# Four-layer network on one core: the expert layer's gathers ordered behind norms, its rows fetched one turn earlier, its one-hots in buffers of their own

## The chip, the core and the metric

The kernel runs on one core of a Trainium2 chip. It is one program of four layers. The metric is the device time of an execution in microseconds; below, "us" counts from the start of the span of the profiled execution. The engines are TensorE (PE, with its weight loads PEld), VectorE (DVE), ScalarE (ACT), GpSimd (POOL) and SyncE (SP, which issues most of the plain DMAs). Each engine executes its own instructions in order, and waits on semaphores for the others.

## The reference

The input x has 4 sequences of 512 tokens of 256 features (`[4, 512, 256]`, here called sequences 0 to 3). Each layer normalises x and adds a mixer and a feed-forward part, both of the same normalised x:

```python
xn = _layernorm(x, axis=-1)
x = x + _L1_attn_ref(xn) + _L1_ffn_ref(xn, ...)
xn = _layernorm(x, axis=-1)
x = x + _L2_attn_ref(xn, ...) + _L2_ffn_ref(xn, ...)
```

The change touches layer 1's end and layer 2's start. Layer 1 has dilated attention (segments of 64 tokens, every second token, 16 heads of 16 features) and a mixture of 32 experts, of which each token takes its best 4:

```python
logits = x @ gate_w.T + gate_b
topk_logits, topk_idx = jax.lax.top_k(logits, K)          # K = 4 of E = 32
topk_weight = jax.nn.softmax(topk_logits, axis=-1)
...                                                        # tokens sorted by expert
gate = jnp.minimum(ragged_dot(xt, w_gate) + b_gate, 7.0)
up = jnp.clip(ragged_dot(xt, w_up) + b_up, -7.0, 7.0)
activated = (up + 1.0) * (gate * sigmoid(1.702 * gate))
outs = ragged_dot(activated, w_down) + b_down
y = sum over the token's 4 experts of outs * topk_weight
```

Layer 2 has a gated linear attention with 16 heads (`_chunk_abc`, weights Wq, Wk, Wv, Wg, Ws, Wo) and a latent attention with 8 experts. Layer 3 is causal attention and another mixture of experts.

## The kernel before

x stays in SBUF as 16 tiles of 128 tokens by 256 features, four to a sequence. `xn` has the same shape and holds the normalised tokens; `xnT` holds them with features on the partitions. The program's order on each engine's queue is fixed when it is built: a scheduler takes the instructions in the order the program emits them, by priorities and by what is ready, so the emitted order of neighbouring pieces shapes each queue but does not set it alone.

**The experts of layer 1.** Tokens are written to DRAM (`l_rows`), each expert's tokens are counted and get places in blocks of 128 rows. Work runs in *units* of two blocks. A unit passes five steps: `fetch1` (two indirect gathers, issued by POOL, bring the rows of its two blocks into a tile `r`, line L1313), `features1` (PE transposes them to rt, L1325; ACT copies to rT), `hidden1` (PE gu L1341, DVE and ACT the activation), `product1` (DVE L1355, L1356), `output1` (PE o L1362, ACT y, SP stores to `l_outs`). `Line.turn` issues, for turn n, the features of unit n, the fetch of a unit ahead, the output of unit n−3, the product of n−2 and the hidden part of n−1. The fetch ahead is of unit n+2 (`at(n + 2)`), into one of three tiles `r`. The arm that runs here has 16 turns of blocks that are given to the experts beforehand and 19 of paired blocks, 35 turns between 215 and 361 us; then an arm of single blocks, 7 turns, 366 to 393 us. Beside the turns run pieces of other work: dilated attention chains, and the building of the four weights of each token (`share1`): one-hots `eq` (DVE compares, POOL multiplies at L1238), which use the tag `pvs` of the dilated chains' ACT copies.

**The end of layer 1.** `collect1(b)` adds the expert results to sequence b: 16 indirect gathers (POOL, L1273), each of 128 rows of 256 from `l_outs`, into eight scratch places lying in `xn` and `xnT` of that sequence, each followed by a DVE multiply-add into x (`accumulate`, L532). `collect1(0)` is interleaved with the last two dilated chains: PE sc L1430, ACT e L1433, PE pv L1442, ACT pvs L1447, PE pvt L1451, DVE r L1453, o L1456 and the add to x L1462. Then `layer_norm(0)`: DVE statistics (L438, L439), POOL rs (L427 and L429, a power of −0.5), DVE xn (L457).

**Layer 2.** `normed(b)` runs what is left of `collect1(b)`, then `layer_norm(b)`, then `to_features` (PE tr L472, ACT xnT). The gated attention goes in units u of a pair of heads and a sequence (u mod 4 is the sequence). `run(u)` interleaves the unit's own steps "m", the supply "s" of unit u+1 (its projections PE pj L1664), the drain "d" of unit u−1, and, beside them, a latent chain. While units 0 to 2 run, one or two gathers of `collects[u + 1]` are emitted per step:

```python
for _ in range(2 - (u and n % 2)):
    next(gathered, None)
```

DVE a L1989 is the latent attention's norm (its rms comes from POOL L427 and L429 as well), eF L1674 the first exponent step of a unit, s L1733 a masked product of scores; kT L2034, q L2040 and L2043 (POOL) and junk L2066 belong to the latent attention; POOL L1828, L1832 and L1835 to the gated output's norm. `rsqrt` remembers its last instruction in `self.mark`, which is POOL's L429.

Of the kernel before, what the change touches and what calls it, by code (L numbers as in the profile page):

```python
# [115 lines left out]
class Net:  # L116
# [934 lines left out]
    def layer1(self):  # L1051
        nc, a, moe, r1 = self.nc, self.a, self.moe1, self.r1
        with ExitStack() as ctx:
            tp = lambda n, bufs, **k: ctx.enter_context(self.tc.tile_pool(name=n, bufs=bufs, **k))
            wp = tp("l1w", 1)

            gw, gb, bg, bu1, bd = self.l1w
            more = wp.tile([P, 8, 3, D], F32, tag="more", name="more")
            self.stock += [more[:, :4], more[:, 4:]]
            for g in (2, 3):  # L1060
                self.load_group(g)
            wa, wk = tp("l1a", 2), tp("l1", 3)
            ptr, pg, po, pd = (tp("l1" + n, 2, space=PSUM) for n in ("tr", "g", "o", "d"))
            self.wk1, self.ps1, self.fetched = wk, (ptr, pg, po), {}

            e = wa.tile([P, 16, 4, 32], F32, tag="e", name="e", bufs=1)
            v = wa.tile([P, 2, 8, 32], F32, tag="v", name="v", bufs=1)
            zeros = lambda n: self.hide.unsqueeze(1).to_broadcast([P, n, T])
            nc.scalar.mul(v.rearrange("p c j d -> p (c j d)").unsqueeze(1), zeros(1), 0.0)
            nc.gpsimd.memset(v[:, :, :, 16:17], 1.0)  # L1070
            nc.scalar.mul(e.rearrange("p (i j) s n -> p i (j s n)", j=4), zeros(4), 0.0)

            units = [(b, p) for b in range(NB) for p in range(2)]
            dilated = lambda u: self.dilated(*units[u], e, v, wa, pd, scalar=u < 2 or u > 5)
            early = [dilated(u) for u in range(2)]
            turns = iter([early[0]] * 3 + [early[1]] * 3)
            for _ in self.places1(wk, po):
                chain = next(turns, None)
                if chain:
                    next(chain)  # L1080
            held = [wp.tile([P, 2, D], F32, tag=f"r{i}", name="r") for i in range(2)]
            for i in range(2):
                self.fetch1(2 * i, held[i])
            for chain in early:
                next(chain)
            bias = self.block_bias(wp, wa, ptr, po, (bg, bu1))

            static = lambda t: dict(place=t % 16, bias=(bg[:, t : t + 1], bu1[:, t : t + 1]))
            over = lambda c: tuple(bias[:, m, c : c + 1] for m in range(2))
            pair = lambda j: [dict(place=j if j < 2 else 8 + (j - 2) % 8, bias=over(j))] * 2  # L1090
            single = lambda j: dict(place=(2 + j) % 8, bias=over(32 + j))

            def static_done(n):
                if n % 2 and n < 8:
                    self.load_group(n // 2 + 4)
                if n == 8:
                    for j in range(2):
                        self.load_expert(j, j)
                if n in (10, 11):
                    for j in range(3 * (n - 10), 3 * (n - 10) + 3):  # L1100
                        self.load_expert(2 + j, 32 + j)
                if n >= 12:
                    for j in range(2 * (n - 12), 2 * (n - 12) + 2):
                        self.load_expert(8 + j, 2 + j)

            singles_at = STATIC + 2 * PAIRS
            for pairs in self.arms1(0, [1 + 2 * i for i in range(PAIRS // 2 + 1)]):
                line = Line(self)
                at = lambda n: 2 * n if n < STATIC // 2 + pairs else None
                pieces = self.beside1(bd, wa, ptr, pd, [dilated(u) for u in (2, 3, 4, 5)])  # L1110
                credit, rate = 0.0, 35 / (STATIC // 2 + pairs - 1)
                for n in range(STATIC // 2):
                    line.turn(
                        dict(t=2 * n, n=n, parts=[static(2 * n), static(2 * n + 1)], done=static_done), at(n + 2)
                    )
                    if n in (8, 10):
                        self.fetch1(singles_at + n - 8, held[n // 2 - 4])
                    credit += rate
                    while credit >= 0.999:
                        credit -= 1  # L1120
                        next(pieces, None)

                def pair_done(j):
                    if 2 <= j < pairs - 8:
                        self.load_expert(8 + (j - 2) % 8, j + 8)

                for j in range(pairs):
                    line.turn(dict(t=STATIC + 2 * j, n=j, parts=pair(j), done=pair_done), at(STATIC // 2 + j + 2))
                    credit += rate
                    while credit >= 0.999:  # L1130
                        credit -= 1
                        next(pieces, None)
                line.end(pieces)
            for singles in self.arms1(1, list(range(17))):
                line = Line(self)

                def single_done(k):
                    for j in (2 * k + 8, 2 * k + 9):
                        if j < 2 * singles:
                            self.load_expert((2 + j) % 8, 32 + j)  # L1140

                for j in (6, 7):
                    if j < 2 * singles:
                        self.load_expert((2 + j) % 8, 32 + j)
                for k in range(singles):
                    line.turn(
                        dict(t=singles_at + 2 * k, n=k, parts=[single(2 * k), single(2 * k + 1)], done=single_done),
                        singles_at + 2 * k + 4 if k + 2 < singles else None,
                    )
                line.end(iter(()))  # L1150
            self.latent_loads()
            last = [dilated(u) for u in (6, 7)]
            next(last[0])
            turns = {1: 0, 4: 0, 5: 1, 8: 1, 10: 0, 12: 1}
            for n, _ in enumerate(self.collect1(0)):
                if n in turns:
                    next(last[turns[n]])
            self.layer_norm(0)
            for chain in last:
                for _ in chain:  # L1160
                    pass
        self.routing.close()
        self.stats = self.small
        self.ordered.close()
# [11 lines left out]
    def beside1(self, bd, wa, ptr, pd, chains):  # L1176
# [54 lines left out]
        for m in range(6):  # L1231
            if m > 1:
                nc.vector.tensor_reduce(self.share1[:, :, m - 2], eqs[m - 2], AX.X, ALU.add)
            if m < 4:
                eq = wa.tile([P, 4, P], F32, tag="pvs", name="eq").rearrange("p a b -> p (a b)")
                eqs.append(eq.rearrange("p (i e) -> p i e", e=32))
                nc.vector.tensor_tensor(eqs[m], slot, s8[:, :, m : m + 1].to_broadcast([P, NTILE, 32]), ALU.is_equal)
                nc.gpsimd.tensor_tensor(eqs[m], eqs[m], w, ALU.mult)  # L1238
            yield
# [66 lines left out]
    def fetch1(self, t, r=None):  # L1306

        nc, moe = self.nc, self.moe1
        if r is None:
            r = self.wk1.tile([P, 2, D], F32, tag="r", name="r")  # L1310
        self.fetched[t] = r
        for i in range(2):
            nc.gpsimd.indirect_dma_start(  # L1313
                out=r[:, i, :], out_offset=None, in_=moe["rows"][:, :],
                in_offset=bass.IndirectOffsetOnAxis(ap=moe["in_slot"][:, t + i : t + i + 1], axis=0),
            )
# [164 lines left out]
    def layer2(self):  # L1481
# [8 lines left out]
        with ExitStack() as ctx:  # L1490
# [19 lines left out]

            def normed(b):
                if b:
                    for _ in collects[b]:
                        pass
                    self.layer_norm(b)
                yield
                self.to_features(
                    gp["ps"], self.xn[:, 4 * b : 4 * b + 4, :], self.xnT[:, :, b * T : (b + 1) * T], tag="ps"
# [3 lines left out]
            def run(u, beside, rate):  # L1522
# [7 lines left out]
                order = "mmmmsmsmmdmmsmsdmsd" if u + 1 < UNITS else "mmmmdmmdmmdmmm"  # L1530
                for n, what in enumerate("mmmmmmmdmmmsmsmdssds" if u < NB - 1 else order):
                    next(chains[what], None)
                    for _ in range(2 - (u and n % 2)):
                        next(gathered, None)
                    credit += rate
                    while credit >= 1:
                        credit -= 1
                        next(beside, None)

            collects = {b: self.collect1(b) for b in range(1, NB)}  # L1540
            norms = [normed(b) for b in range(NB)]
            for it in (norms[0], supplied(0)):
# [982 lines left out]
```

## Time and profile before

| | us |
|---|---|
| three timed runs | 2213.72, 2217.41, 2217.51 |
| median | 2217.41 |
| profiled execution, its own time | 2224.51 |
| span of the profiled execution | 2222.8 |
| PE busy in the span | 1959.6 (88%) |
| DVE busy | 1188.3 (53%) |
| ACT busy | 833.8 (38%) |
| POOL busy | 641.3 (29%) |
| gathers of layer 1's results (L1273), 64, first and last start | 397.7, 512.8 |
| one such gather on POOL, median | 0.94 to 0.96 |

The page of a profile gives busy times of the engines, then the span in 40 equal slices with the busy share of each engine in tenths; the chain that ended last; the groups of instructions with the idle time before them and what ended it; and the DMA issues. Beside the page, the trace answers for a window, a line or a tile of the program: what it waited for, and who waited for it. A line such as "POOL rs L429" names engine, tile and line of the kernel.

### The profile page before, as it was taken

Reading aid. Unit: us, or ns where it says so; the run is one execution under the profiler, and the core shown is the slowest. Engines: PE = TensorE matmul, PEld = TensorE weight load, DVE = VectorE, ACT = ScalarE, POOL = GpSimd, SP = SyncE. Lnnn points to the kernel's source line nnn. Section 1 sums busy time; section 2 is a strip of 40 time slices with the busy share of each in tenths; the row PEclk is TensorE's granted clock in tenths of the full one; section 3 lists DMA queues with packets and bytes.
Section 4 is the critical chain, followed back from the end, with each engine's and each line's share of the span. In section 5 each row is a group of like instructions: output and inputs, shape, how many; then the busy total and the mean of one; then the engine's idle time right before and its main releaser. Section 6 shows DMA issues by size and latency. Waiting matters only on the chain.

```text
span 2222.8 us, 35354 instructions
## 1 busy us (share of the span) xinstructions
PE 1959.6 (88%) x13015; PEld 1432.5 (64%) x13015; DVE 1188.3 (53%) x3448; ACT 833.8 (38%) x1681; POOL 641.3 (29%) x748
## 2 busy tenths in 40 slices
PE   5755988158999999999999999999999988899995
PEld 2423877134666676666666676666787866678895
DVE  5747764257465655555555656555655564522223
ACT  1243354221434433434433434334344533334321
POOL 6324573553112112121111121111444352022231
PEclk9955999568999999999999999999899999899998
DMA  8312985430000000000000000001443320167697
GB/s 287 130 38 83 289 257 164 138 90 20 1 18 6 8 11 6 8 10 6 6 13 6 8 11 6 27 11 41 131 125 111 99 81 1 42 229 266 213 329 244
DMA packets 149548, 198.20 MB, mean 89 GB/s; under 512 B 16885, under 2 KB 127576, under 8 KB 149208
## 3 DMA queue, kind: packets, MB, share of 16 engines
q1 hardware_dynamic: 135224, 156.40, 21.8%
q0 software_dynamic: 14112, 39.15, 6.0%
q8 instruction: 111, 1.82, 0.3%
q14 instruction: 101, 0.83, 0.1%
HBM read 154.21 MB, written 41.29 MB: 88 GB/s over the span
## 4 chain that ended last, share of the span: by engine, by line
PE 55%; issue 8%; DVE 8%; POOL 6%; DMA 3%; ACT 2%; another core or an unknown queue 1%; SPq 0%; POOLq 0%; DVEq 0%; ACTq 0%
PE pt L1742 8%; PE pj L1664 6%; PE o L1855 4%; PE kq L2091 3%; PE sc L1727 3%; PE pov L1806 2%; PE g L2276 2%; PE qk L2059 2%; DVE junk L2066 2%; PE pv L2107 2%; DMA r<-l_rows,in_slot 2%; POOL l_outs L383 1%; PE turn L1695 1%; PE st L1715 1%
## 5 line engine op out<-in xcount | busy, mean ns | idle before, releaser
L2066 DVE CUSTOM_DVE_ANT_0 junk<-qk,hide 128x512 f32<-128x512 f32 (+3 forms) x256 | 124.1, 485 | 42.8 <-PE qk L2059 24.5
L2099 POOL TENSOR_SCALAR_AFFINE_SELECT pr<-pr 128x512 f32<-128x512 f32 x64 | 40.3, 642 | 346.6 <-ACT pr L2096 346.6
L2276 PEld LDWEIGHTS g<-rT,we 128*128 128x128 f32 x1120 | 132.2, 194 | 5.3 <-ACT rT L376 3.3
L2276 PE MATMUL g<-rT,we 128*128 128x128 f32 x1120 | 133.0, 278 | 1.7 <-ACT rT L376 1.6
L1742 PE MATMUL pt<-Wg,xnT 128*128 128x256 f32 x512 | 126.9, 401 | 2.6 <-DVE both L361 1.0
L343 POOL DMA_INDIRECT r<-l_rows,in_slot x73 | 71.2, 975 | 191.2 <-PE rt L374 109.0
L383 POOL DMA_INDIRECT l_outs<-y,to x73 | 72.7, 995 | 184.1 <-ACT y L382 152.4
L1855 PE MATMUL o<-Wo,oT 128*128 128x256 f32 x512 | 121.9, 381 | 0.0
L1742 PE MATMUL pt<-Wv,xnT 128*128 128x256 f32 x512 | 120.6, 387 | 0.0
L1733 DVE TENSOR_TENSOR s<-sc,keep 128x512 f32<-128x512 f32 x128 | 82.4, 682 | 66.1 <-PE sc L1727 66.1
L1742 PEld LDWEIGHTS pt<-Wg,xnT 128*128 128x128 f32 x512 | 99.6, 201 | 27.6 <-issue 7.7
L1677 DVE RECIPROCAL rz<-rz 128x128 f32<-128x128 f32 x128 | 116.7, 932 | 0.3
L355 DVE TENSOR_TENSOR mine<-r,number 128x2 f32<-128x2 f32 x73 | 12.8, 175 | 182.0 <-DMA r<-l_rows,in_slot 175.7
L2096 ACT ACTIVATE pr<-kq 128x512 f32<-128x512 f32 (+1 forms) x192 | 86.6, 530 | 53.1 <-PE kq L2091 52.8
L1742 PEld LDWEIGHTS pt<-Wv,xnT 128*128 128x128 f32 x512 | 95.2, 191 | 15.4 <-issue 0.3
L1313 POOL DMA_INDIRECT r<-l_rows,in_slot x84 | 84.5, 1005 | 66.7 <-PE rt L1325 37.3
L1855 PEld LDWEIGHTS o<-Wo,oT 128*128 128x128 f32 x512 | 96.2, 197 | 9.2 <-issue 1.2
L2091 PE MATMUL kq<-q,kT 32*128 32x128 f32 (+3 forms) x512 | 90.3, 485 | 9.7 <-DVE mx L2066 8.1
L1745 ACT COPY v<-pt 128x512 f32<-128x512 f32 x64 | 37.5, 586 | 121.8 <-PE pt L1742 120.7
L2043 POOL TENSOR_TENSOR q<-q 128x512 f32<-128x512 f32 x16 | 20.3, 1267 | 214.4 <-DVE q L2040 214.3
L1823 DVE TENSOR_TENSOR o<-pov,g 128x512 f32<-128x512 f32 x64 | 41.2, 685 | 74.5 <-ACT sq L1822 74.3
L2091 PEld LDWEIGHTS kq<-q,kT 32*128 32x128 f32 x512 | 40.0, 189 | 55.8 <-DVE mx L2066 34.4
(560 smaller groups left out, 4591.9 us busy)
## 6 DMA issues: line engine op xcount, KB each, us to landing
we<-l_w SPq DMA_DIRECT2D x70, 512.0 KB
we<-l_wo SPq DMA_DIRECT2D x35, 512.0 KB
l_outs<-none SPq DMA_DIRECT2D x1, 11776.0 KB
l_outs<-y SPq DMA_DIRECT2D x42, 256.0 KB
we<-l_r_gate SPq DMA_DIRECT2D x38, 128.0 KB
we<-l_r_up SPq DMA_DIRECT2D x38, 128.0 KB
we<-l_r_down SPq DMA_DIRECT2D x38, 128.0 KB
l_rows<-xn SPq DMA_DIRECT2D x8, 544.0 KB
```

The lines of the kernel that those rows point to most:

```text
L343: self.nc.gpsimd.indirect_dma_start(out=r[:, m, :], out_offset=None, in_=moe["rows"][:, :], in_offset=bass.IndirectOffsetOnAxis(ap=moe["in ...
L383: self.no_order(moe["name"] + " back", nc.gpsimd.indirect_dma_start(out=moe["outs"][:, :], out_offset=bass.IndirectOffsetOnAxis(ap=to, axi ...
L1313: nc.gpsimd.indirect_dma_start(out=r[:, i, :], out_offset=None, in_=moe["rows"][:, :], in_offset=bass.IndirectOffsetOnAxis(ap=moe["in_slot ...
L1664: nc.tensor.matmul(ps, w[n][:, k, :], self.xnT[:, k, t["b"] * T : (t["b"] + 1) * T], start=(k == 0), stop=(k == KD - 1))
L1677: inverse = lambda c: nc.vector.reciprocal(rz[:, c * P : (c + 1) * P], rz[:, c * P : (c + 1) * P])
L1733: nc.vector.tensor_tensor(s, ps[hh], keep4, ALU.mult)
L1742: nc.tensor.matmul(ps[:, i, :], self.xnT[:, k, s : s + P], w[n][:, k, :], start=(k == 0), stop=(k == KD - 1))
L1855: nc.tensor.matmul(ps[:, p, :], of_parity(oT[:, h, c * D : (c + 1) * D], p), wo[:, h, :], start=(h == 0), stop=(h == 1),)
L2066: nc.vector.tensor_tensor_reduce(out=junk[:, :m], in0=tiles[j][:, off : off + m], in1=self.hide[:, T - m :], op0=ALU.add, op1=ALU.max, sca ...
L2091: nc.tensor.matmul(tiles[j][:, BLOCK[i] - off : BLOCK[i] - off + T - i * P], kT[r, i * P : (i + 1) * P], qT[r, i * P :], start=True, stop= ...
L2096: nc.scalar.activation(pr[:, j, off : off + m], tiles[j][:, :m], AF.Exp, scale=0.25)
L2276: nc.tensor.matmul(pt[:, m, :], we[:, q, k * T + m * P : k * T + (m + 1) * P], rT[:, k, :], start=(k == 0), stop=(k == KD - 1),)
```

## The change

It has three parts. In the arm of pairs the rows are fetched three turns ahead in place of two, with one more fetch at the start and four tiles `r`. The one-hots `eq` get a tag of their own. And the gathers of sequences 1 to 3 in layer 2 are emitted inside `issue_after(marks[...])`: the scheduler puts them, with what they emit, behind the marked instruction, which is the rs of the norm of the preceding sequence. Nothing of what is computed changes, and the number of gathers is the same.

```diff
             for pairs in self.arms1(0, [1 + 2 * i for i in range(PAIRS // 2 + 1)]):
                 line = Line(self)
+                self.fetch1(4)
                 at = lambda n: 2 * n if n < STATIC // 2 + pairs else None
...
                     line.turn(
-                        dict(t=2 * n, n=n, parts=[static(2 * n), static(2 * n + 1)], done=static_done), at(n + 2)
+                        dict(t=2 * n, n=n, parts=[static(2 * n), static(2 * n + 1)], done=static_done), at(n + 3)
                     )
...
-                    line.turn(dict(t=STATIC + 2 * j, n=j, parts=pair(j), done=pair_done), at(STATIC // 2 + j + 2))
+                    line.turn(dict(t=STATIC + 2 * j, n=j, parts=pair(j), done=pair_done), at(STATIC // 2 + j + 3))
...
             if m < 4:
-                eq = wa.tile([P, 4, P], F32, tag="pvs", name="eq").rearrange("p a b -> p (a b)")
+                eq = wa.tile([P, 4 * P], F32, tag="eq", name="eq")
                 eqs.append(eq.rearrange("p (i e) -> p i e", e=32))
...
         if r is None:
-            r = self.wk1.tile([P, 2, D], F32, tag="r", name="r")
+            r = self.wk1.tile([P, 2, D], F32, tag="r", name="r", bufs=4)
         self.fetched[t] = r
...
             def normed(b):
                 if b:
-                    for _ in collects[b]:
-                        pass
+                    with self.tc.issue_after(marks[b - 1]):
+                        for _ in collects[b]:
+                            pass
                     self.layer_norm(b)
+                marks.append(self.mark)
                 yield
...
-                    for _ in range(2 - (u and n % 2)):
-                        next(gathered, None)
+                    with self.tc.issue_after(marks[min(u, NB - 1)]):
+                        for _ in range(2 - (u and n % 2)):
+                            next(gathered, None)
                     credit += rate
...
+            marks = []
             collects = {b: self.collect1(b) for b in range(1, NB)}
```

## The prediction

> **What bounds the kernel now.** I read the page first, then the ten-microsecond windows round the weakest slices, then the chain, the waits and POOL's own timeline there. The first line of the page and the tenths of PE:
>
> ```profile
> span 2222.8 us, 35354 instructions
> PE 1959.6 (88%) x13015; PEld 1432.5 (64%) x13015; DVE 1188.3 (53%) x3448; ACT 833.8 (38%) x1681; POOL 641.3 (29%) x748
> ...
> PE   5755988158999999999999999999999988899995
> ```
>
> PE is the bound nearly everywhere. One slice (the eighth, 389 to 445 us) has a 1: the end of layer 1 and the start of layer 2. The windows of that place:
>
> ```profile
> 400.00:410.00 10.00, 3.01 (x48) 1.95 (x48) 3.05 (x8) 2.40 (x5) 7.69 (x8) 0.50 0.95 330
> 410.00:420.00 10.00, 0.00 (x0) 0.00 (x0) 3.15 (x7) 0.00 (x0) 7.56 (x9) 0.50 0.48 134
> 420.00:430.00 10.00, 0.00 (x0) 0.00 (x0) 3.42 (x8) 0.00 (x0) 8.47 (x9) 0.50 0.36 104
> ...
> 450.00:460.00 10.00, 0.15 (x1) 0.00 (x0) 2.04 (x7) 0.00 (x0) 7.79 (x10) 0.50 0.33 98
> 460.00:470.00 10.00, 8.47 (x20) 4.39 (x21) 6.23 (x22) 4.19 (x13) 7.76 (x8) 0.70 0.75 225
> ...
> 550.00:560.00 10.00, 10.00 (x54) 6.62 (x53) 4.86 (x10) 4.38 (x8) 1.26 (x1) 1.00 0.00 0
> ```
>
> After the bounds come the length, then PE, PEld, DVE, ACT and POOL busy, the granted clock, the DMA share and GB/s. PE stands still while POOL is the busiest engine; from 540 us on PE is full, so time won before that is kept to the end. The waits from 390 to 480 us:
>
> ```profile
> ACT pvs L1447 <- remote: 32.8, 1, 32.8
> ...
> DVE r L1453 <- PE pvt L1451: 15.8, 1, 15.8
> ...
> PE tr L472 <- DVE xn L457: 10.9, 1, 10.9
> ...
> DVE xn L457 <- POOL rs L429: 8.6, 1, 8.6
> ```
>
> And POOL's timeline, first with the gathers (L1273) of sequence 0, last with the norm of sequence 0:
>
> ```profile
> 397.67 0.95 POOL L1273 DMA_INDIRECT xn<-l_outs,at  x1 [20.33 <-DMA l_outs<-y]
> ...
> 416.99 0.95 POOL L1273 DMA_INDIRECT xnT<-l_outs,at  x1 [0.30 <-issue]
> 418.24 0.94 POOL L1273 DMA_INDIRECT xn<-l_outs,at  x1 [0.30 <-issue]
> ...
> 446.38 0.95 POOL L1273 DMA_INDIRECT xnT<-l_outs,at  x1 [8.89 <-DVE x L532]
> ...
> 456.99 0.95 POOL L1273 DMA_INDIRECT xnT<-l_outs,at  x1 [0.31 <-issue]
> 458.01 0.20 POOL L427 TENSOR_SCALAR rs<-mv 128x4 f32<-128x4 f32 x1
> 458.48 0.99 POOL L1273 DMA_INDIRECT xnT<-l_outs,at  x1 [0.27 <-issue]
> 459.50 1.05 POOL L429 TENSOR_TENSOR rs<-rs,neghalf 128x4 f32<-128x4 f32 x1
> ```
>
> Layer 2 starts when norm 0's rs is out: T0 = 459.50 + 1.05 = 460.55; DVE xn follows at 460.59, PE tr at 461.05. Two things hold T0. First, POOL's queue: between the last gather of sequence 0 (416.99) and rs stand all 16 of sequence 1 and 7 of sequence 2, though norm 0 needs none of them. Second, the one long piece of 32.8 us "remote": PE's last pv of a dilated chain ran at 404 to 406, but ACT read it only at 437.09; DVE, in order, then stood before r L1453 until 443.61 and had norm 0's statistics at 451.27. No engine's work explains this piece, and it may belong to the profiled execution alone.
>
> **How the profiled run stands to the times.** It took 2224.51 us, span 2222.8, the three timed runs 2213.72, 2217.41 and 2217.51: 7.1 above their median. Without the 32.8 us, POOL's queue alone would set T0: 39 gathers at the pitch of 1.255 (418.24 to 419.49, and so on) are 48.9, two memsets of the `both` tile 2.1, from 397.67 to 448.7; then rs L427 with its gaps 0.5, one more gather 1.3, rs L429 1.05: T0 about 451.6, 9.0 earlier than profiled. 2224.5 − 9.0 = 2215.5, among the timed runs. So I take the timed runs to be without that piece, and bound by POOL's queue here.
>
> **The change part by part.** *Gathers behind the norm before them.* The instruction order after the change has POOL as: 16 gathers of sequence 0, two memsets, rs, rs; then sequence 1's 16; norm 1's rs, rs; sequence 2's; norm 2's; sequence 3's. Removed ahead of norm 0's L429 are 24 gathers (16 + 7 + the one between), 24 × 1.255 = 30 us of POOL. What is late next is sequence 0's own last gather: issued 416.99, added (L532) 2.8 to 3.4 us later where DMA is a third busy (418.24 gives the add at 421.68), 5.8 to 6.4 where its share was 0.95 (404.02 gives 410.47); I take 3.4, the share being 0.48 to 0.36 by then: 420.4. The add 0.5, the last statistics 2.5 (448.00 to 451.27 is 3.3, with three adds of other sequences between that go), rs 0.2 + 0.2 + 1.05: T0 = 425.1. PE's pvt, which DVE needs before its last six adds, is ready by 412.5 (ACT pvs 0.6, q 3.4, two sc of 1.1 after 406.3). Gain: 451.6 − 425.1 = 26.5 against the timed runs, 35.4 against the profiled one. With slow landings T0 is 428.
>
> *What is put behind the norms.* Every gather still runs, now after the mark, and SP's order stays. Behind T0 stand 16 gathers of sequence 1 (20.1 us of POOL) with norm 0's side branch among them: rms L429 came at 474.12 (T0 + 13.6) behind 9 gathers, and now comes behind 12, T0 + 16.5. Waiting for it in the old order was DVE a L1989 (8.39), and eF L1674 behind that, at T0 + 15.9. In the new order eF stands ahead of a, behind seven adds: the seventh gather at T0 + 7.7, landed + 3.4, eF at T0 + 11.1. From here DVE s L1733 is as before (T0 + 22 to 24). Norm 1 waits for sequence 1's last gather: T0 + 36 to 38.5, where it was T0 + 36; unit 1's pj L1664 needs PSUM that DVE s frees, T0 + 51 in both. Sequence 2's gathers come after norm 1: their adds stand in DVE's queue before kT L2034, which goes from T0 + 57.6 to about T0 + 62.3, and holds PE's unit 1: +4.7. Sequence 3's 16 adds (0.4 each, 6.4 us of DVE) and the two q L2043 that POOL now does behind gathers (1.27 each) mostly meet a full PE. I take +5.5; ends +3 (all of it but 3 covered) and +12 (all 6.4 uncovered as well).
>
> [...]
>
> *Rows three turns ahead.* In the arm of 19 pairs (215 to 361 us) the same 74 gathers are issued, one turn earlier, into four buffers. What could go:
>
> ```profile
>   DMA r<-l_rows,in_slot: 10.1, 7
> ```
>
> from the view of PE's rt L1325: idle until the rows came, PE 4.3 in three pieces and its weight loads 5.8 in four, the same moments in part, 5.7 us in all, between 276 and 293 us. There POOL had stood 7.8 us before its multiplication eq L1238, waiting for DVE, with the fetches queued behind; one unit more now stands ahead of each. POOL's wait for free row buffers (37.3 us, released by PE rt) costs nothing while PE has rows. Ends 0 (DVE is 9.9 of 10 busy in 270 to 280 and is late next) and 5.7; I take 3. The first extra fetch costs POOL two issues, 2.5 us, at the arm's start, while PE has the rows of the turns before. In the singles' arm the distance stays.
>
> *Own one-hot buffers.* eq and pvs shared two buffers; the first pvs of the arm came at 302, the last eq was done by 291. No wait to remove: nothing, and no instruction more.
>
> Sum on the timed runs: 2217.4 − 26.5 + 5.5 − 3 = 2193.4; against the profiled run 2224.5 − 35.4 + 5.5 − 3 = 2191.6. With slow landings 3 more. I forecast 2195.
>
> **Rivals.** *The 32.8 us piece ends with the gathers.* If it is real and hangs on POOL's 32 gathers in a row (it ends at 437.1, the last of the run starts at 436.53), it ends after 16 of them, near 419. Then q 3.4, two sc, pvt, DVE r at 426, six adds and statistics: T0 about 434, 8 later than 426: 2202. For it: the coincidence; against: the timed runs fit without it.
>
> *The piece is real and stays.* DVE r stays at 443.61; o, x and adds 3.9, statistics 2.3, rs 1.5: T0 = 451.3, 9.2 less than profiled. 2224.5 − 9.2 + 5.5 − 3 = 2217.8 for a profiled run, and 2211 to 2218 for timed ones. For it: it is in the only trace; semaphore steps near it are slow too. Against: 2213.7.
>
> *Slower: late adds hold DVE.* DVE is in order, and each sequence's adds now land some 20 us of POOL later, in between the attention's DVE work. Place: unit 1 and 2, 480 to 560 us, DVE already 7 to 9 of 10 busy. If eF, s and kT each wait for the last gather ahead of them (20.1 for one sequence's issues + 3.4) in units 1 and 2 instead of 4.7 once, the price is 2 × 23.5 − 4.7 = 42, against 26.5 + 3: 2217 + 8, about 2225. It decides from about 35 us of added wait. Against: the order shows most of these adds behind, not ahead of, the steps that PE waits for.
>
> *Nothing of the row fetch pays* adds 3 to any case and is within each range.
>
> **How the numbers follow.** Forecast 0.55 (2187 to 2203, from T0 425 to 428, +3 to +12, and 0 to −5.7); piece ending with the gathers 0.16 (2196 to 2209); piece staying 0.18 (2210 to 2219); DVE held 0.11 (above 2219). The range 2186 to 2217 leaves out the last case, part of the third and the forecast's very edge. A measurement of this kernel tells about 0.2%, 4.4 us, from no change: faster means under 2213. The first two cases are faster, 0.71, and with 0.07 of the third 0.78; same 0.10, of the third; slower 0.12, the last case and 0.01 of the third.
>
> **What would show it.** POOL's rs L427 directly behind sequence 0's gathers and memsets, near 424; PE tr L472 near 426 in place of 461; the 8.6 us of DVE xn for rs gone; eF about 11 us behind T0; kT some 62 behind; rt's 10.1 us for rows shrunk; the first window with PE at 10.00 some 20 us earlier than 540. Wrong it would be if T0 stays past 445, or PE's idle time between T0 and 560 grows by over 15 us.

## The result and the profile after

The changed kernel took 2204.23 us (median of six runs, 2198.98 to 2207.6) against 2216.89 for the kernel before (six runs, 2213.72 to 2220.5). The ratio is 0.9942, 95% interval 0.9924 to 0.996: 12.7 us or 0.58% faster, where 2195 was forecast. Its profiled execution took 2200.35 us, span 2198.6.

T0, the end of norm 0's rs, moved as forecast. POOL's timeline of the changed kernel, with the idle time before an instruction and its releaser in brackets (L1274 is the gather that was L1273):

```profile
395.27 0.94 POOL L1274 DMA_INDIRECT xn<-l_outs,at  x1 [22.51 <-DMA l_outs<-y]
...
414.46 1.08 POOL L1274 DMA_INDIRECT xnT<-l_outs,at  x1 [0.30 <-DVE x L1463]
415.54 1.82 POOL L1941 MEMSET both<- 128x2048 f32 x1
417.42 0.38 POOL L1942 MEMSET both<- 128x64 f32 x1
421.05 0.20 POOL L427 TENSOR_SCALAR rs<-mv 128x4 f32<-128x4 f32 x1 [3.25 <-DVE mv L439]
421.33 1.04 POOL L429 TENSOR_TENSOR rs<-rs,neghalf 128x4 f32<-128x4 f32 x1
422.57 1.19 POOL L1274 DMA_INDIRECT xn<-l_outs,at  x1 [0.20 <-issue]
```

Sequence 0's 16 gathers, the two memsets, then rs, which now waits 3.25 us for DVE's statistics: POOL's queue is no longer what ends last. T0 is 421.33 + 1.04 = 422.37 (forecast 425.1, before 460.55). PE's wait for DVE xn fell from 10.9 to 5.2. DVE xn's for rs fell from 8.6 to 2.9, in two pieces of 1.5, one of norm 0 and one of norm 1:

```profile
POOL rs L427 <- DVE mv L439: 9.8, 2, 6.5
...
PE tr L472 <- DVE xn L457: 5.2, 1, 5.2
...
DVE xn L457 <- POOL rs L429: 2.9, 2, 1.5
```

The ten-microsecond windows of the changed kernel (length; PE, PEld, DVE, ACT, POOL busy; granted clock, DMA share, GB/s) answer to those shown of before:

```profile
410.00:420.00 10.00, 3.05 (x36) 2.23 (x36) 8.65 (x21) 2.02 (x4) 6.53 (x7) 0.50 0.38 109
420.00:430.00 10.00, 6.65 (x14) 3.52 (x15) 4.44 (x15) 3.84 (x12) 7.14 (x8) 0.50 0.51 143
...
450.00:460.00 10.00, 10.00 (x52) 6.58 (x51) 6.80 (x20) 6.56 (x16) 4.43 (x6) 1.00 0.10 27
...
490.00:500.00 10.00, 7.09 (x16) 4.16 (x17) 10.00 (x23) 0.63 (x1) 8.36 (x8) 0.50 0.31 92
500.00:510.00 10.00, 10.00 (x34) 5.85 (x34) 3.95 (x12) 1.77 (x3) 5.97 (x7) 0.50 0.19 54
...
520.00:530.00 10.00, 10.00 (x58) 6.35 (x57) 9.20 (x20) 2.54 (x6) 1.26 (x1) 1.00 0.00 0
```

Read two columns together here. PE is full from 500 us on, 40 us earlier than in the profile before; but in 500 to 510 the clock is 0.50 and 34 matmuls are done, in 520 to 530 it is 1.00 and 58 are done. A full PE at half clock is where most of the missing part of the gain went, as the experiments show.

### The profile page after: what moved, and what is told of

It is laid out like the page before. It is cut to its first block, busy times and chain, and to the rows that moved or that the text cites. A ratio compares the mean times of both kernels' runs of the same rounds, so it can differ in the third digit from the quotient of the medians.

```text
span 2198.6 us, 35345 instructions
## 1 busy us (share of the span) xinstructions
PE 1973.0 (90%) x13015; PEld 1439.7 (65%) x13015; DVE 1196.7 (54%) x3448; ACT 833.7 (38%) x1681; POOL 640.4 (29%) x748
## 4 chain that ended last, share of the span: by engine, by line
PE 57%; DVE 9%; issue 5%; POOL 5%; DMA 4%; ACT 1%; SPq 0%; POOLq 0%; DVEq 0%; another core or an unknown queue 0%; ACTq 0%
PE pt L1747 8%; PE pj L1669 6%; PE g L2281 5%; PE o L1860 4%; PE kq L2096 3%; PE sc L1732 3%; PE pov L1811 3%; PE qk L2064 2%; PE o L2294 2%; PE pv L2112 2%; DVE junk L2071 2%; DMA r<-l_rows,in_slot 2%; PE turn L1700 1%; PE st L1720 1%; PE qkp L2372 1%
```

## The experiments: the parts apart

The runs came in three sets, each on one chip. Each ratio is against the kernel before in the same set (medians 2214.23, 2235.74 and 2214.5 us), so times of different sets aren't compared. All profiles are compared in one way: T0, and the time from T0 to one and the same instruction, the one that the second profile of the kernel before had reached at 600 us, where PE is full again.

**The kernel before, profiled again**, to see whether the 32.8 us "remote" piece is always there.

> The kernel before, profiled once more. If the piece of 32.8 us (ACT pvs, remote, ending at 437) belongs to that one profiled execution, it is gone here, norm 0's rs L429 ends at 450 to 453 behind the gathers of sequences 1 and 2, and the run takes 2213 to 2218. If it is real and belongs to the kernel, it is there again with rs ending near 460.

Measured: 2213.86 us, and no such piece. ACT read PE's pv at once, and POOL's queue set T0:

```profile
402.99 0.58 ACT L1447 COPY pvs<-pv 128x512 f32<-128x512 f32 x1 [2.05 <-PE pv L1442]
```

```profile
445.52 0.94 POOL L1273 DMA_INDIRECT xnT<-l_outs,at  x1 [0.30 <-issue]
446.54 0.19 POOL L427 TENSOR_SCALAR rs<-mv 128x4 f32<-128x4 f32 x1
447.00 0.99 POOL L1273 DMA_INDIRECT xnT<-l_outs,at  x1 [0.27 <-issue]
448.02 1.05 POOL L429 TENSOR_TENSOR rs<-rs,neghalf 128x4 f32<-128x4 f32 x1
```

T0 is 449.07, where the prediction worked out 451.6 for a run without the piece. From sequence 0's first gather to T0 it is 53.6 us here and 422.37 − 395.27 = 27.1 in the changed kernel: 26.5 us won at POOL's queue, the forecast term to a tenth.

**The gathers' order alone** (the changed kernel without the row fetch and without the one-hots' tag, of which the row fetch's core is shown).

```diff
-                self.fetch1(4)
...
-                        dict(t=2 * n, n=n, parts=[static(2 * n), static(2 * n + 1)], done=static_done), at(n + 3)
+                        dict(t=2 * n, n=n, parts=[static(2 * n), static(2 * n + 1)], done=static_done), at(n + 2)
...
-            r = self.wk1.tile([P, 2, D], F32, tag="r", name="r", bufs=4)
+            r = self.wk1.tile([P, 2, D], F32, tag="r", name="r")
```

> Only the third part of the change: the gathers of sequences 1 to 3 behind the norm before them; rows two turns ahead and shared buffers as before. If POOL's queue ahead of norm 0's rs is what the change takes away, rs L429 ends 25 to 30 us earlier than the 451.6 worked out for before, near 424 to 426, no long remote piece is needed for it, and the whole is 9 to 12 us faster than before (about 2206), nearly all of the change's 12.7. If the row fetch made most of it, this one is within 4 us of before.

Measured: 0.9928 (0.9898 to 0.9957), first gather to T0 26.9 us. The first gather and norm 0's rs:

```profile
400.84 0.94 POOL L1273 DMA_INDIRECT xn<-l_outs,at  x1 [20.43 <-DMA l_outs<-y]
...
426.68 1.04 POOL L429 TENSOR_TENSOR rs<-rs,neghalf 128x4 f32<-128x4 f32 x1
```

The order of the gathers carries the change: its ratio lies within the interval of the whole change's.

**The row fetch alone** (the lines above put into the kernel before).

> Only the first part: rows fetched three turns ahead with four tiles r. By the trace of after, PE's lag in the pair arm moves from +1.2 us at 260 to -2.7 us from 300 on, so 3 to 4 us less at 393 us, POOL's first gather of layer 1's results near 394 to 395, and 2 to 4 us in the time (ratio 0.998 to 0.999). If the row fetch only uses cover that is there already, 0; if the larger tile pool moves other work, it can be slower.

Measured: 0.997 (0.9945 to 0.9996). Against the second profile of before, the same PE instructions come 0.4 us earlier in 220 to 260, 2.2 in 300 to 350, and a steady 3.6 to 3.7 from 380 to 1700 us; the forecast term was 3. The wait it removes, in the view of PE's rt of the kernel before (second profile), 215 to 361 us:

```profile
  DMA r<-l_rows,in_slot: 10.8, 7
```

No such line is left in the changed kernel, whose list for rt there begins so:

```profile
  issue: 8.8, 6
```

**The one-hots' tag alone.**

```diff
-                eq = wa.tile([P, 4, P], F32, tag="pvs", name="eq").rearrange("p a b -> p (a b)")
+                eq = wa.tile([P, 4 * P], F32, tag="eq", name="eq")
```

> Only the second part: the one-hots eq in buffers of their own. No wait is removed by the trace, so within 2 us of before (ratio 0.999 to 1.001). If the shared buffers cost something that the trace does not name, POOL's multiplication eq L1238 or ACT's pvs come earlier and up to 3 us are won.

Measured: 1.0008 (0.9971 to 1.0045). Nothing, as forecast. But its profile has the "remote" piece again, 35.7 us of it on ACT, ending 3.5 us after POOL's last gather of the run started (second fence, POOL's timeline):

```profile
439.70 0.59 ACT L1447 COPY pvs<-pv 128x512 f32<-128x512 f32 x1 [35.66 <-remote]
```

```profile
434.98 0.95 POOL L1273 DMA_INDIRECT xnT<-l_outs,at  x1 [0.30 <-issue]
436.24 0.96 POOL L1273 DMA_INDIRECT xnT<-l_outs,at  x1 [0.30 <-issue]
```

**The changed kernel, profiled again in that set.**

> The changed kernel, profiled once more. T0 422 to 424 again. If the slow clock behind the 7.3 us wait belongs to this order of instructions, it is there again, with 20 to 30 us lost to the clock between T0 and the full stretch; if it was chance, it is near the 13 to 15 of the two profiles of before, and this run is some 10 us faster.

Measured: 0.9913 (0.9883 to 0.9942). Here the piece is in the changed kernel too, but shorter:

```profile
423.09 0.59 ACT L1448 COPY pvs<-pv 128x512 f32<-128x512 f32 x1 [14.82 <-remote]
```

```profile
418.26 0.95 POOL L1274 DMA_INDIRECT xnT<-l_outs,at  x1 [0.30 <-issue]
419.51 0.95 POOL L1274 DMA_INDIRECT xnT<-l_outs,at  x1 [0.30 <-issue]
```

Of 14 profiles five show it: the first of before, and all four of the second set. Each time ACT reads pv 0.6 to 3.8 us after POOL starts the last of a run of gathers: 32.8 to 35.7 us of waiting with 30 gathers in the run, 14.7 and 14.8 with 16 (two memsets stand among the 30, and behind the 16). In all five POOL then has nothing to do: its next instruction, a gather or rs, waits for DVE, and DVE stands behind this very pv. So where the piece occurs it ends about when POOL runs out of work, and the change shortens it by over half: T0 goes from 463.15 (the tag alone) to 437.36, 25.8 us, or 28.6 if both are counted from their first gather, about what POOL's queue gives in the runs without it. That the gathers hold the signal is not shown by this. Why PE's signal reaches ACT so late in some executions and not in others is open.

**Sequence 1's gathers set free**, those of sequences 2 and 3 left behind their norms, to give POOL's queue ahead of rs a middle dose.

```diff
-                    with self.tc.issue_after(marks[b - 1]):
+                    with self.tc.issue_after(marks[b - 1]) if b > 1 else ExitStack():
...
-                    with self.tc.issue_after(marks[min(u, NB - 1)]):
+                    with self.tc.issue_after(marks[min(u, NB - 1)]) if u else ExitStack():
```

> The changed kernel, but the gathers of sequence 1 may come before norm 0 as they did; only those of sequences 2 and 3 are held back. POOL then has 32 gathers ahead of norm 0's rs. If POOL's queue alone sets T0, rs L429 ends 16 x 1.25 = 20 us behind the changed kernel's, near 441 to 442 (it was 449 with 39 and two in between). If something else does (DVE, the landing of sequence 0's gathers), it stays near 424. With norm 1 then ready at once, the time should lie between the two, 2208 to 2213.

Measured: 0.9975 (0.9946 to 1.0004), T0 458.26. The piece is there with 30 gathers in the run (35.6 us, to 442.53; the other two of the 32 wait for DVE behind it), and rs waited for DVE's statistics behind it, not for POOL's queue. So the dose that was wanted was not given; what the run shows is the piece at its old length with the old run of gathers.

## The experiments: where the rest of the gain went

T0 came 26.5 us earlier and the kernel ended 12.7 us earlier. The ledger from T0 to the same instruction, through the same 750 matmuls. "Lost to the clock" is worked out from windows of 1 us: PE busy times (1 − granted clock), summed.

| profile | T0 | from T0 | PE busy | PE idle | lost to the clock |
|---|---|---|---|---|---|
| before, second | 449.07 | 150.9 | 129.5 | 21.4 | 13.4 |
| before, first (with the piece) | 460.55 | 154.6 | 131.2 | 23.3 | 15.3 |
| rows alone | 445.24 | 151.1 | 129.8 | 21.3 | 13.8 |
| tag alone (piece) | 463.15 | 154.4 | 130.9 | 23.5 | 14.9 |
| changed | 422.37 | 169.2 | 144.8 | 24.4 | 25.5 |
| changed, second (piece) | 437.36 | 164.8 | 139.5 | 25.3 | 20.8 |
| changed, third | 420.21 | 169.6 | 143.3 | 26.3 | 24.2 |
| gathers' order alone | 427.73 | 173.4 | 147.9 | 25.5 | 30.3 |
| sequence 1 free (piece) | 458.26 | 161.7 | 138.9 | 22.8 | 20.0 |

The view of windows for the second of before and for the changed kernel, one line each:

```profile
449.07:600.00 150.93, 129.49 (x750) 80.95 (x750) 94.81 (x237) 48.21 (x99) 45.72 (x49) 0.88 0.11 32
```

```profile
422.37:591.59 169.22, 144.83 (x750) 88.30 (x750) 102.79 (x252) 48.42 (x99) 68.85 (x74) 0.82 0.16 47
```

The changed kernel gives back 18.3 us, of which 3.0 is idle time of PE and 15.3 is the same matmuls taking longer; the clock accounts for 12.1 of the 15.3. Position tells which: up to the first exponent of unit 1, eF, the distance from T0 grew from 63.5 to 69.2 us, 5.7; the other 12.5 came between there and the full stretch. That place, first the second profile of before, then the changed kernel:

```profile
512.00:523.00 11.00, 9.04 (x22) 4.62 (x23) 10.68 (x29) 0.65 (x2) 4.79 (x4) 0.53 0.00 0
523.00:543.00 20.00, 20.00 (x137) 13.63 (x136) 10.33 (x30) 5.54 (x12) 1.26 (x1) 1.00 0.00 1
```

```profile
485.00:515.00 30.00, 22.70 (x61) 13.03 (x60) 21.87 (x57) 2.70 (x5) 20.57 (x22) 0.50 0.20 57
```

Before, PE worked 9 us at about half clock and then had the full clock; changed, it worked 22.7 us at 0.50. With the gathers' order alone it is 27.8, in the second and third profiles of the changed kernel 27.1 and 23.3. What precedes it is one wait for the latent attention's DVE mx, longer in the changed kernel (first line) than before (second fence):

```profile
PE qk L2064 <- DVE mx L2071: 7.3, 1, 7.3
```

```profile
PE qk L2059 <- DVE mx L2066: 4.2, 1, 4.2
```

But a long wait alone doesn't do it. The second profile of before has a longer one, at layer 2's start, with only about 4 us of PE's work at half clock behind it:

```profile
PE tr L472 <- DVE xn L457: 19.6, 1, 19.6
```

In before the full clock came back after 4 and 9 us of PE's work at half clock, here only after 22.7 to 27.8: as much busy time did not bring it back.

The shapes of the matmuls tell what is different. In a form such as `32*128 32x384` the first number is how many of the array's 128 rows a matmul feeds, the second how many of its columns it uses, the last how many columns it streams. First the second profile of before, then the changed kernel:

```profile
513.87 5.65 PE L2059 MATMUL qk<-kT,q 32*128 32x384 f32 x16 [4.16 <-DVE mx L2066]
519.46 3.49 PE L1664 MATMUL pj<-xnT,Wq 128*128 128x512 f32 x4
```

```profile
496.92 2.08 PE L1669 MATMUL pj<-xnT,Wq 128*128 128x512 f32 x2
498.93 2.07 PE L2064 MATMUL qk<-kT,q 32*128 32x384 f32 x4
500.93 2.08 PE L1669 MATMUL pj<-xnT,Wq 128*128 128x512 f32 x2
...
505.98 1.65 PE L1732 MATMUL sc<-qT,kT 64*128 64x128 f32 x12
507.56 1.22 PE L2064 MATMUL qk<-kT,q 32*128 32x256 f32 x2
...
512.59 2.88 PE L1747 MATMUL pt<-Wv,xnT 128*128 128x256 f32 x6
```

In all 14 profiles the granted clock is 0.50 or 1.00, and it stays at 0.50 for whole multiples of 3.41 us, but for the stretch that ends each program. Cut these times into pieces of 3.41 us, and count in each piece columns × rows / 128 (at most PE's busy share, since matmuls on part of the array's columns ran side by side: at half clock 16 of sc L1431, `128*32 128x128`, took 1.08 us, four of turn L1700, `128*128 128x128`, 1.06). Four matmuls of 128 rows and 512 columns, whose starts lie 0.85 us apart at half clock, fill a piece. Leaving out the one that ends each program, the clock rose at the end of 451 pieces, and each of these was at least 0.74 full. Of the 957 pieces at whose end it stayed down, 903 were less than 0.74 full, though PE was busy throughout in 149 of them. In the changed kernel the five pieces from 494.8 to 511.9 have PE busy throughout and are 0.53, 0.45, 0.68, 0.66 and 0.66 full: qk with 32 rows and sc with 64 run in between the matmuls of 128 rows. The next is 0.76 full, and the clock comes back. In the second profile of before the qk ran in one go (0.13, 0.34), and the piece behind it is 0.89 full. So in these five pieces PE was busy throughout and kept the half clock, while much of its work fed few rows. This is a count over the records; no run here varied the rows alone. The runs below tried other causes.

**All later gathers behind norm 0 only**, so that no gather waits for norms 1 and 2. The theory that the later norms' marks cost the give-back expects a shorter stretch.

```diff
-                    with self.tc.issue_after(marks[b - 1]):
+                    with self.tc.issue_after(marks[0]):
...
-                    with self.tc.issue_after(marks[min(u, NB - 1)]):
+                    with self.tc.issue_after(marks[0]):
```

> The changed kernel, but the gathers of sequences 2 and 3 only have to come behind norm 0, as sequence 1's do, not behind norms 1 and 2. T0 should be as after (about 422). If what after gives back behind T0 (some 14 us between T0 and 590 us in the profiles) is the late adds of sequences 2 and 3 in DVE's order, this gives 5 us or more of it back: 2195 to 2200. If it is DVE's and PE's own order around unit 1 or the clock, the time stays within 4 us of 2204.

Measured: 1.0016 (0.9998 to 1.0033), although T0 is 420.16. Norm 1's rs, with POOL's queue ahead of it again, came at T0 + 49.6 in place of T0 + 33.3:

```profile
467.70 0.99 POOL L1274 DMA_INDIRECT xnT<-l_outs,at  x1 [0.27 <-issue]
468.70 1.05 POOL L429 TENSOR_TENSOR rs<-rs,neghalf 128x4 f32<-128x4 f32 x1
```

But the stretch from T0 is 169.8 (23.7 lost to the clock), as in the changed kernel, so the marks of norms 1 and 2 do not make the give-back. The time is lost later, with the same order of instructions: in 1400 to 1600 us PE is as busy as in the changed kernel, at a lower clock, with 8% fewer matmuls (changed first). The same matmul comes 3.7 us later than in the changed kernel at 1400 and 14.6 later at 1600:

```profile
1400.00:1600.00 200.00, 188.60 (x1254) 139.00 (x1253) 115.97 (x400) 80.28 (x158) 48.40 (x58) 0.93 0.20 61
```

```profile
1400.00:1600.00 200.00, 189.42 (x1152) 133.63 (x1149) 110.43 (x383) 75.59 (x147) 42.23 (x52) 0.87 0.17 52
```

**The same kernel once more**, to see whether that is chance.

> All gathers behind norm 0 only, profiled once more. The first profile was as good as after to 600 us and lost 13 us between 1400 and 1520 and 9 us near 1800 to 1840 against it, at a granted clock of 0.87 in place of 0.93, with the same instructions in the same order. If these losses belong to this kernel's timing, they are there again; if they are chance, this run is 10 to 20 us faster against the kernel before than the first.

Measured: one execution, 2221.33 us; T0 423.47, 173.2 from T0, and the low clock at the same place again:

```profile
1400.00:1600.00 200.00, 189.23 (x1170) 132.89 (x1169) 109.35 (x374) 73.07 (x142) 42.19 (x51) 0.87 0.17 54
```

It belongs to that kernel. The changed kernel's second and third profiles have 0.91 there, the second of before 0.92. Why a shift in layer 2 sets the clock a thousand microseconds later is open.

**The wait filled**: eight idle matmuls ahead of the qk that waits, so that PE would not stand still before the half-clock run.

```diff
+                    if c == 3 and j == 3 and not lp.get("filled"):
+                        lp["filled"] = True
+                        for _ in range(8):
+                            nc.tensor.matmul(tiles[j], self.ident, lp["aT"][:, 0, :], start=True, stop=True)
```

> The changed kernel with eight idle multiplications of 128x128 by 512 columns (0.9 us each at full clock) put into PE's order in the first maxima step of the latent attention, behind the qk L2064 that ends at 485.6 us, where PE then waits 7.3 us for DVE mx. Their result is overwritten, nothing else is computed differently. If the clock is what takes back the gain (granted 0.50 from 486 to 515 us behind that wait, 25.5 us of PE's time between T0 and the full stretch lost to it, against 13.4 in the kernel before), the clock stays at 1 there, the loss falls to 15 or less, and the time falls by 5 to 12 us below the changed kernel's. If the slow clock has another cause, or DVE's queue sets the pace of that stretch, the time stays within 3 us of the changed kernel's or rises by up to the 7 us of the fill.

Measured: 0.9956 (0.9928 to 0.9984), slower than the changed kernel in its set (0.9913); 177.6 us from T0, of which 29.7 idle and 21.8 lost to the clock. The scheduler moved DVE's order with the new matmuls, and another wait for mx grew to 10.6 us. The run tells nothing of the filled wait by itself. (The 0.9 us expected of each idle matmul is not that of the full clock: in the changed kernel four matmuls of 128 rows and 512 columns took 1.88 us at a granted clock of 1.00, pj L1669 at 431.19, their starts 0.43 apart. So the eight are about 3.4 us there, an estimate from these starts, not 7.)

**Fewer late adds**: 24 of the 32 adds of sequences 2 and 3 left out, the gathers kept, for the rival that DVE's adds hold unit 1.

```diff
-                self.accumulate(i, y, self.share1[:, i, m : m + 1])
+                if b < 2 or m < 1:
+                    self.accumulate(i, y, self.share1[:, i, m : m + 1])
```

> The changed kernel without 24 of the 32 adds of sequences 2 and 3 (three of each token's four experts are left out; the gathers stay). 24 x 0.4 = 9.6 us of DVE go between T0 + 35 and T0 + 110. If the late adds in DVE's order are what makes PE wait and the clock drop, the stretch from T0 to the same point falls from 165 to 169 us to 155 or less, and the loss to the clock to 13 to 16. If they are covered, the stretch shortens by less than 4 us. The later layers see other data, so the whole time says nothing here.

Measured: one execution, 2210.88 us; 171.2 us from T0, no shorter, with 10.4 us less of DVE work:

```profile
422.49:593.72 171.23, 139.22 (x750) 86.35 (x750) 92.38 (x229) 47.95 (x98) 68.27 (x73) 0.84 0.16 47
```

DVE's work on the late adds is not what the stretch is made of. The order moved here as well: PE's idle time is 32.0 in place of 24.4, its loss to the clock 19.8 in place of 25.5. The last gather of this kernel starts at 501.8, and the clock stays at half until 526, so the end of the gathers doesn't bring the clock back either.

**Sequence 3's gathers later still**, behind POOL's last multiplication of unit 0: they start at T0 + 76.5 in place of T0 + 64.8, so that none of them lies in the first part of the half-clock place.

```diff
-                    with self.tc.issue_after(marks[min(u, NB - 1)]):
+                    with self.tc.issue_after(self.scaled[0] if u == 2 else marks[min(u, NB - 1)]):
...
+            mark = nc.gpsimd.tensor_tensor(
...
+        self.scaled.append(mark)
```

> The changed kernel, but sequence 3's gathers come behind unit 0's scaling o (POOL L1840, 502 us in the profile of after) in place of norm 2's rs (487 us). POOL then does unit 0's rs and o 10 us earlier, and 4 adds leave DVE's crowded stretch of unit 1. If the late gathers and adds set what unit 1 loses, the stretch from T0 to 590 us (169 us in after, 151 in before) gets 3 to 8 us shorter and the time 0.1 to 0.4 per cent less than the changed kernel's. If only the slow clock behind the 7 us wait sets it, the stretch stays within 3 us, since that wait (PE qk for DVE mx) comes before all of sequence 3.

**The changed kernel a third time**, beside it.

> The changed kernel once more, to be compared with seq3_later on the same chip. T0 to the full stretch 164 to 170 us, 20 to 26 of them lost to the clock, if the loss belongs to this order of instructions.

Measured: 0.9908 (0.9873 to 0.9943; 2198.92 us) for sequence 3 later and 0.9936 (0.9902 to 0.997; 2205.43) for the changed kernel. From T0 it is 166.2 against 169.6; the half-clock run in unit 1 holds 10 us of PE work in place of 23, but a later one holds 14 in place of 10, and the sum lost to the clock is the same, 24.5 against 24.2. By the medians it is the best kernel here; the intervals overlap, so that isn't settled.

## Why the prediction was right or wrong

**What held T0.** Right. "POOL's queue alone would set T0" at 451.6: measured 449.07. The gain of 26.5 at T0: measured 26.5. "What is late next is sequence 0's own last gather": rs waits 3.25 us for its statistics. (The terms listed for T0 add up to 424.9, not 425.1; from the first gather to T0 that is 27.2, and 27.1 was measured.)

**The 32.8 us piece.** "It may belong to the profiled execution alone" is half right: the second profile of before lacks it, but it comes back in other executions. Where it does, the first rival's rule holds in size: forecast to end near 419 after 16 gathers and to give T0 about 434, it ended at 423.09 and gave 437.36, with a first gather 2.5 us later. Its "32 gathers in a row" were 30; the next gather waited for DVE. "The piece is real and stays" fell: with 16 gathers it is under half as long. The semaphore steps near it that were called slow: in its profile the next pvs came 1.02 us after PE's pv had ended (447.37 to 448.39), in the changed kernel's 0.06 us after (415.88 to 415.94). The gain at T0 is about the same with it, which the prediction did not see: 25.8 us between two kernels that both have it.

**What is put behind the norms.** This is the step that failed: "I take +5.5; ends +3 (...) and +12". The mechanism it listed is there in size. Sequence 1's adds hold eF to T0 + 13.0 (forecast 11.1), the second kT is 5.2 us farther from T0 (forecast 4.7), and unit 1's eF 5.7. Slow landings are there, while weights load (Wv, Wg and Wo, issued by SP from 423.92 to 426.87): 3.1 us from the first gather's start to its add, 6.7 from that of the fourth (426.59), at a DMA share of 0.86:

```profile
424.00:434.00 10.00, 9.04 (x21) 4.10 (x19) 3.15 (x10) 4.08 (x13) 7.64 (x8) 0.70 0.86 262
```

```profile
433.30 0.48 DVE L532 SCALAR_TENSOR_TENSOR x<-xn,share,x 128x256 f32<-128x256 f32 x1 [2.01 <-DMA xn<-l_outs,at]
```

What the sum left out is the clock: it priced waits and took every matmul's duration as before. The term measured 18.3 us between two profiles without the piece (10.4 between two that have it: 164.8 − 154.4), and of the 18.3 12.1 are loss to the clock. It is three times the forecast and above its upper end of 12. With 18.3 in its place the sum is 2217.4 − 26.5 + 18.3 − 3 = 2206.2; the median was 2204.23. That lies between the ends of the forecast's own case (its terms add up to 2188 and 2206, where it states 2187 and 2203) only because the ends of the other terms made room; the size of this term was not foreseen. The sign to look for, "PE's idle time between T0 and 560 grows by over 15 us", could not have caught it: idle time grew by 3.0.

**Norm 1.** "T0 + 36 to 38.5, where it was T0 + 36" was wrong for the kernel before: there norm 1's rs came at T0 + 15.6, in the changed kernel at T0 + 33.3. It fell into slack: unit 1's eF moved by 5.7, not 18.

**The slower rival**, DVE held by late adds, 42 us: not seen. (Its sum is wrong as well: 42 against 29.5 is 12.5 slower, about 2230, not 2225.) The adds hold eF and kT by a few microseconds each, and leaving three quarters of sequences 2 and 3's out shortened nothing.

**The rows and the one-hots.** Forecast 3 and 0; measured 3.6 to 3.7 between profiles for the rows, and a ratio of 1.0008 for the one-hots. On top of the gathers' order the rows' share can't be told from the times (0.9928 without, 0.9942, 0.9913 and 0.9936 with, in different sets).

## What to carry to other kernels

A tiny operation at the end of an in-order queue of transfers can set when a whole layer starts: rs, 1.05 us of POOL behind the gathers, ended at 449.07 in the second profile of before and at 422.37 in the changed kernel; reordering that queue gave at T0, to half a microsecond, what counting its instructions said. But time won before a stretch isn't kept through it because PE is "full" there: split the time between the same two instructions into PE's idle time, its work at full clock and its loss to the clock, since busy time alone calls a half-speed PE full (10.00 of 10 us busy here, with 34 matmuls at a clock of 0.50 and with 58 at 1.00). Look at how many rows the matmuls there feed (here five pieces with PE busy throughout were 0.45 to 0.68 full). And profile the old kernel twice before you reason on a stall: one profile showed 32.8 us that the next did not have.

## What the runs showed of the hardware that was not expected

- A signal from PE to ACT that ACT saw only about when POOL's run of gathers ended: 14.7 to 35.7 us, in five of 14 profiles, longer with 30 gathers than with 16.
- In 14 profiles the clock rose at the end of 451 pieces of 3.41 us, each at least 0.74 full by the count of columns × rows (the least full 0.76 in the changed kernel's profile, 0.79 in the first of before). At the end of 149 pieces less than 0.74 full, in which PE was busy throughout, it stayed at 0.50.
- PE 22 to 29 us busy at a granted clock of 0.50 before the clock came back, in six of the ten profiles with later gathers; at most 9 us in the four with the old order.
- Two kernels that differ only in layer 2's start differ in the clock 1000 us later: 0.93, 0.91 and 0.91 in 1400 to 1600 us in three profiles of the one, 0.87 in both of the other.
